# Two chained cross-attentions: layer-0 queries in blocks of 4, 8, 8, 6 and 6 subtiles instead of four blocks of 8

## The chip, the core and the metric

The kernel runs on one core of a Trainium2 chip. The metric is the device time of one execution in microseconds (us). A core has a matrix engine (PE in the profile, with its weight loads as PEld), a vector engine (DVE), an activation engine (ACT), GpSimd (POOL) and SyncE (SP), which here issues nearly all transfers. Each engine executes its own list of instructions in order and waits on semaphores; 16 DMA engines move data between DRAM and on-chip memory.

## The reference, cut to what matters

```python
# x: (4, 1024, 1024), context: (4, 64, 1024), all float32
# layer 0: 32 query heads of 32, 8 key/value heads
q = x @ Wq + bq; k = ctx @ Wk + bk; v = ctx @ Wv + bv
scores = einsum(q, k) / sqrt(32) + mask
out = softmax(scores) @ v
x1 = layernorm(out @ Wo + bo + x) * gamma + beta
# layer 1: 16 heads of 64, keys and values from layernorm(ctx)
Q = x1 @ Wq1.T; K = a @ Wk1.T; V = a @ Wv1.T
out = softmax(where(mask, Q K^T / 8, -inf)) @ V
y = x1 + tanh(gate) * (out @ Wo1.T)
```

There are 4096 query rows. The context is so short (256 rows in all) that layer 1 never forms Q: the keys are multiplied into Wq1 (the "folding of queries": matrices `ad`, one per batch) and the values into Wo1 (matrices `bd`), and layer 1 is then two 1024-by-1024 products per row.

## The kernel before, in words

**Units.** A subtile is 128 query rows; there are 32 (`NSUB`). A block is 8 subtiles (`SUB`), so 1024 rows, and there are 4 blocks (`NBLK`). Every large product is done by a Strassen-like scheme with 7 half-size products in place of 8: the left matrix is held as A11, A12, A22 and sums S1 to S4, the right as B11, B21, B22 and T1, T2, T3, N4.

**Layer-0 queries of one block.** `rows0(blk)` turns the rows of x into the 7 right-hand pieces of a block, each 512 columns wide: 8 DVE transposes (`turn_quarters`, L376) from the row buffers `xq`, then 4 DVE sums (L170 to L173). It returns three steps that are hung behind steps 22, 25 and 26 of the block before ("fills"). `query_steps(blk, rows)` gives 28 steps, 4 output slices times 7 products; a product is 4 matmuls at L536 (each shown by the profile as 2 rows). `keep` copies a PSUM bank to SBUF with the bias on ACT (L544), `add` adds a second bank on DVE (L550), and `put` sends the slice to DRAM (`qTd`, L547, on the SP queue). The SBUF tiles that `keep` writes (`e`, `z`, `u`, `f`) have two buffers each.

**Layer-0 attention of one subtile.** `attend0(t)` loads the queries of the subtile back from `qTd` (L593) and does, in two halves, scores (PE, L604), scaling and mask (DVE, L609), row maxima, subtraction, exponent (DVE L453 and L461, ACT L462), sums and division (DVE L471, L472, L476). `outputs0(t)` transposes the probabilities (PE L633, ACT L634), multiplies by the values (PE L639, ACT L643) and writes the result to `oTd` in DRAM (L645). A subtile can start only when the whole of its block's queries is in `qTd`.

**Mixing.** `mix(t, others)` writes the attention of subtile t, the outputs of subtile t-1 and a few other steps among each other. Block 0's queries are computed alone. After that the attention of block b is mixed with the 28 query steps of block b+1, 3 or 4 steps to a subtile: one step at each of four places, the rest behind the values.

```python
    for blk in range(NBLK - 1):
        steps = query_steps(blk + 1, rows)
        ...
        for i in range(SUB):
            lo, hi = i * 7 // 2, (i + 1) * 7 // 2
            mix(blk * SUB + i, steps[lo:hi] if i < SUB - 1 else steps[lo:])
```

The attention of the last block is mixed with the folding of layer-1 queries, one of 8 chunks to a subtile (`folded_queries`: a transposed weight chunk, PE L370 and ACT L371; 16 matmuls, L737; 8 evictions on ACT, L743; two writes of 1 MB to `ad`, L749). The chunk, its transpose and the two results take buffers from a ring of 7 (`wb`). The same stretch loads Wo of layer 0 and makes its sums (`w_o_sums`). This stage is called the fold stage below; the three before it are called mixed stages 0, 1 and 2.

**What follows.** 16 pairs of subtiles go through Wo and layer 1 (`project`, L400). For each pair `load_outputs` fetches the attention outputs from `oTd` (L782) and the residual rows, and `left_out` makes the sums S1 to S4 of them.

**Order.** The program gives each step in the order of the text; a scheduler then orders every engine's instructions by its own estimate of when their inputs are ready, and the order is fixed from there. So an engine can stand at an instruction whose input is late while a later one would be ready. Rows of x are loaded through `more_rows`: four row buffers for the first two blocks, two for the later ones, refilled as they come free, on the same SP queue as `put`.

Of the kernel before, what the change touches and what calls it, by code (L numbers as in the profile page):

```python
# [8 lines left out]
F32 = mybir.dt.float32  # L9
U8 = mybir.dt.uint8  # L10
AF = mybir.ActivationFunctionType
# [9 lines left out]
L = 1024  # L21
S = 64
NTOK = B * L
SUB = 8
TB = SUB * P
HT = TB // 2
NSUB = NTOK // P
NBLK = NTOK // TB
NPAIR = NSUB // 2
Q = 32  # L30
NQ = P // Q
# [35 lines left out]
def tile_two_cross_attentions(  # L67
# [47 lines left out]

    x1 = [dram.tile([2 * P, H], F32, tag=f"x1_{t}", name=f"x1_{t}") for t in range(NPAIR)]
    p1 = [dram.tile([2 * P, H], F32, tag=f"p1_{t}", name=f"p1_{t}") for t in range(NPAIR)]
    oTd = [dram.tile([P, KC, 2 * P], F32, tag=f"oT_{t}", name=f"oTd_{t}") for t in range(NPAIR)]
    qTd = [dram.tile([P, KC, TB], F32, tag=f"qT_{t}", name=f"qTd_{t}") for t in range(NBLK)]
    v0d = dram.tile([B * S, 256], F32, tag="v0d", name="v0d")  # L120
    kTd = dram.tile([P, KC, B * S], F32, tag="kTd", name="kTd")
    vTd = dram.tile([P, KC, B * S], F32, tag="vTd", name="vTd")
# [108 lines left out]
        for a in range(NQ):  # L231
            queue.dma_start(out=t[a * Q : (a + 1) * Q], in_=v[a])

    order = [(blk, i) for blk in range(NBLK) for i in range(4)]
    ahead = []
    free = [4, 2]

    def more_rows():

        while order and free[order[0][0] > 1]:  # L240
            blk, i = order.pop(0)
            free[blk > 1] -= 1
            xq = xpools[blk > 1].tile([P, 2 * NQ, QW], F32, tag="x", name=f"xq{blk}_{i}")
            at = blk * TB + i * 2 * P
            load_quarters(xq, x[at : at + 2 * P, :])
            ahead.append(xq)

# [132 lines left out]

    def left_out(o, pool, name):

        a11, a21 = o[:, 0:HK, 0:P], o[:, 0:HK, P : 2 * P]
        a12, a22 = o[:, HK:KC, 0:P], o[:, HK:KC, P : 2 * P]
# [5 lines left out]
        return {"A11": a11, "A12": a12, "A22": a22, "S3": a21, **s}  # L390

    def project(a, w, r, fill, bias=None, tail=None):

# [102 lines left out]
    def rows0(blk):  # L496

        r = {
            n: new_block("wb", f"x{n}_{blk}") for n in ("B11", "B21", "T1", "B22", "T3", "T2", "N4")
        }  # L500

        sums = right_sums(r)
        taken = []

        def turn_into(name, xq, i, h):
            at = slice(i % 2 * 2 * P, (i % 2 + 1) * 2 * P)
            turn_quarters(xq, r[name][:, :, at], (h * HK, (h + 1) * HK))

        def first_half():
            for i in range(2):  # L510
                xq = ahead.pop(0)
                turn_into("B11", xq, i, 0)
                turn_into("B21", xq, i, 1)
                done_with_rows(blk)

        def b12():
            for i in range(2, 4):
                taken.append(ahead.pop(0))
                turn_into("T1", taken[-1], i, 0)
            sums[0]()  # L520

        def b22():
            for i in range(2, 4):
                turn_into("B22", taken.pop(0), i, 1)
                done_with_rows(blk)
            run(sums[1:])

        return r, {22: first_half, 25: b12, 26: b22}

    def query_steps(blk, rows):  # L530

        tmp = {}

        def product(bank, a, b, i, first, last):
            for k in range(HK):
                nc.tensor.matmul(  # L536
                    bank, w_q[a][:, k, sub_ap(i)], rows[b][:, k, :],
                    start=first and k == 0, stop=last and k == HK - 1, skip_group_check=True,
                )

        def keep(name, bank, i, h):
            t = tmp[name] = etmp.tile([P, HT], F32, tag=name, name=f"{name}_{blk}_{i}")
            m = h * HK + i
            nc.scalar.activation(t, bank, AF.Identity, bias=bq_sb[:, m : m + 1])  # L544

        def put(name, i, h, u):
            nc.sync.dma_start(out=qTd[blk][:, h * HK + i, u * HT : (u + 1) * HT], in_=tmp[name])  # L547

        def add(name, bank, i, h, u):
            nc.vector.tensor_tensor(tmp[name], bank, tmp[name], ALU.add)  # L550
# [38 lines left out]
    def attend0(t):  # L589

        b = t * P // L
        q = qpool.tile([P, KC, P], F32, tag="q", name=f"q0_{t}")
        nc.sync.dma_start(out=q, in_=qTd[t // SUB][:, :, sub_ap(t % SUB)])  # L593
# [26 lines left out]
    def outputs0(t):  # L620
# [15 lines left out]
        def values(c):  # L636
            ps = one()
            for i in range(2):
                nc.tensor.matmul(  # L639
                    ps[i * 64 : (i + 1) * 64, :], v0bd[:, b, c, i, :], pTs[c][:, i, :],  # L640
                    start=True, stop=True,
                )
            nc.scalar.copy(oT[:, c * 4 : (c + 1) * 4, :].rearrange("p g l -> p (g l)"), ps)  # L643
            if c == 1:
                nc.sync.dma_start(out=oTd[t // 2][:, :, sub_ap(t % 2)], in_=oT)  # L645

        return flip, values

    def mix(t, others):

        front, back = attend0(t)
        o = iter(others)

        def other():
            step = next(o, None)
            if step:
                step()

        front(0)
        other()  # L660
# [11 lines left out]
        if t:  # L672
            values(0)
            values(1)
        for step in o:
            step()

    rows, fills = rows0(0)
    run(fills.values())
# [15 lines left out]
    for blk in range(NBLK - 1):  # L695
        steps = query_steps(blk + 1, rows)
        if blk + 2 < NBLK:
            rows, fills = rows0(blk + 2)

            def both(n, fills=fills, steps=steps):  # L700
                steps[n]()
                if n in fills:
                    fills[n]()

            steps = [lambda n=n: both(n) for n in range(28)]
        for i in range(SUB):
            lo, hi = i * 7 // 2, (i + 1) * 7 // 2
            mix(blk * SUB + i, steps[lo:hi] if i < SUB - 1 else steps[lo:])
    queries_cm.close()


# [66 lines left out]
        return [lambda bp=bp: keys(bp) for bp in range(2)]  # L778

    def load_outputs(pair):  # L780
        o = (o2pool if pair else early).tile([P, KC, 2 * P], F32, tag="o2", name=f"o2_{pair}")
        nc.sync.dma_start(out=o, in_=oTd[pair])  # L782
        r = []
        for u in range(2):
            t = pair * 2 + u
            ru = (rpool.tile([P, H], F32, tag="r", name=f"r_{t}") if pair
                  else early.tile([P, H], F32, tag="r", name=f"r_{t}", bufs=2))
            nc.sync.dma_start(out=ru, in_=x[sub_ap(t), :])
# [3 lines left out]

    kT = fold.tile([P, KC, B * S], F32, tag="kvT", name="kT")
    nc.sync.dma_start(out=kT, in_=kTd)
    wch = chunk(wq1, 0, "wq1")
    w_o, w_o_sums = right_weight(wo0, "wa", "wo0")
    bo_sb = constant(bo0.partition_broadcast(P), [P, H], "bo", F32, fold)
    for i in range(SUB):
        ahead = chunk(wq1, i + 1, "wq1") if i + 1 < KC else None
        mix((NBLK - 1) * SUB + i, folded_queries(kT, wch, i))  # L800
        wch = ahead
        if i == 3:
            run(w_o_sums)
        if i == 5:
            first_outputs = load_outputs(0)
    flip, values = outputs0(NSUB - 1)
    for part in (flip, values):
# [38 lines left out]
    def turn_x1(pair, xq, pool=None, tag="xT"):  # L846
# [4 lines left out]
            turn_quarters(xq, xT[:, h * HK : (h + 1) * HK, :], (h * HK, (h + 1) * HK))  # L851

        def blocks():
            lefts[pair] = left_out(xT, lpool if pool else lxpool, f"x_{pair}")

        return [lambda: half(0), lambda: half(1), blocks]

# [49 lines left out]
    def score(pair, fill):  # L907
        if pair:
            s = [spool.tile([P, H], F32, tag="s", name=f"s1_{pair}_{u}") for u in range(2)]
        else:  # L910
            both = o2pool.tile([P, 2, H], F32, tag="o2", name="s1_0")
            s = [both[:, u] for u in range(2)]
# [30 lines left out]
    def turn_at_once(pair):  # L943
        pT = new_pT(pair)
        del scores[pair]
        for u in range(2):
# [4 lines left out]
        return left_out(pT, lppool, f"p_{pair}")  # L951

    probs1 = {}
    at_once = {}
# [1 line left out]
    def turn_p(pair):  # L956
# [7 lines left out]
            turn_quarters(pq, pT[:, h * HK : (h + 1) * HK, :], (h * HK, (h + 1) * HK))  # L964

        def blocks():
            probs1[pair] = left_out(pT, lppool, f"p_{pair}")

        return [lambda: half(0), lambda: half(1), blocks]

# [93 lines left out]
```

## Time and profile before

| | us |
|---|---|
| median of 3 runs | 1969.04 (1968.19 to 1970.54) |
| the profiled execution, its own time | 1970.75 |
| its span in the trace | 1969.0 |
| start: context, keys and values | 0 to 83.1 |
| block 0's queries alone, up to block 1's first product | 83.1 to 178.0 |
| mixed stage 0 (8 subtiles, 28 steps of block 1) | 178.0 to 330.2 |
| mixed stage 1 | 330.2 to 482.1 |
| mixed stage 2 | 482.1 to 629.5 |
| fold stage (8 subtiles, 8 chunks) | 629.5 to 749.4 |
| Wo of layer 0 and layer 1 | 749.4 to 1969.0 |

The stage bounds are the starts of the first product of the next block, and in the last two rows the end of the last query product and the first product at L400. The profiled execution took 1.7 us more than the median run and its span is 1.75 us under its own time; a change of the span can be carried to the median as it is. Matrix products dominate, PE is busy in 98% of the span; but an engine can be busy and yet wait in small pieces, so the stages have to be read one by one.

### The profile page before, as it was taken

To read this page: it belongs to the slowest core of one execution; us is meant where nothing else is said; L and a number is where in the kernel's file an instruction comes from. 1 tells how busy PE (TensorE), PEld (TensorE's weight loads), DVE (VectorE), ACT (ScalarE), POOL (GpSimd) and SP (SyncE) were. 2 spreads that over 40 slices of the span, in tenths; PEclk is the share of its full clock that TensorE was granted. 3 is DMA by queue.
4 is the path that set the end of the run, shared out by engine and by line. 5 is a ranking of instruction groups with operands and counts; after the bars stand their busy time and mean duration, and the time that the engine had idled before them with its cause. 6 is when DMAs were issued, how large, how long until landed. Compare 5 with 4: busy or idle time off the path is not lost.

```text
span 1969.0 us, 16487 instructions
## 1 busy us (share of the span) xinstructions
PE 1929.0 (98%) x6208; PEld 922.9 (47%) x6208; DVE 1273.0 (65%) x1540; ACT 348.6 (18%) x564; POOL 237.6 (12%) x103
## 2 busy tenths in 40 slices
PE   8999999999999999999999999999999999999999
PEld 7744554444454664444443444444444444444443
DVE  3504968598877993455467667657675766576653
ACT  1011333243333672212200000000000000000000
POOL 0000000000000102445455643000000000000000
PEclk9999999999999899999999999999999999999999
DMA  8972226234425888376483335455746574747421
GB/s 276 181 178 71 90 82 161 72 110 120 128 89 192 278 268 288 136 238 226 157 247 119 118 109 126 139 145 154 181 118 161 138 181 118 179 120 181 118 86 43
DMA packets 204559, 301.17 MB, mean 153 GB/s; under 512 B 19136, under 2 KB 134208, under 8 KB 201920
## 3 DMA queue, kind: packets, MB, share of 16 engines
q1 hardware_dynamic: 185216, 270.75, 48.1%
q10 hardware_dynamic: 19264, 29.37, 5.4%
q8 instruction: 49, 0.80, 0.2%
q14 instruction: 30, 0.25, 0.0%
HBM read 182.37 MB, written 117.70 MB: 152 GB/s over the span
## 4 chain that ended last, share of the span: by engine, by line
PE 89%; DVE 8%; DMA 1%; issue 1%; ACT 1%; SPq 0%; DVEq 0%; ACTq 0%
PE wx L400 58%; PE wx L536 17%; PE big L604 2%; PE one L639 2%; PE one L633 2%; DVE s L609 1%; PE wx L350 1%; PE one L350 1%; DVE mx L453 1%; DVE s L461 1%; PE one L764 1%; DVE sm L471 1%; DVE s L476 1%; PE wx L737 1%; PE big L764 1%
## 5 line engine op out<-in xcount | busy, mean ns | idle before, releaser
L408 DVE TENSOR_TENSOR r<-wx,r 128x512 f32<-128x512 f32 x224 | 153.9, 687 | 269.3 <-PE wx L400 262.7
L462 ACT ACTIVATE s<-s 128x1024 f32<-128x1024 f32 x96 | 101.7, 1060 | 748.0 <-DVE s L461 739.3
L789 POOL TENSOR_TENSOR r<-r,bo 128x1024 f32<-128x1024 f32 x32 | 79.1, 2476 | 820.6 <-DMA r<-in_x_dram 819.5
L412 DVE TENSOR_TENSOR s<-wx,key_bias 128x512 f32<-128x512 f32 x64 | 44.2, 690 | 136.9 <-PE wx L400 136.9
L471 DVE TENSOR_REDUCE sm<-s 128x16 f32<-128x1024 f32 x96 | 115.2, 1211 | 22.0 <-ACT s L462 21.5
L536 PE MATMUL wx<-xT,wq_S 128*128 128x512 f32 x256 | 118.9, 605 | 3.1 <-DVE xT L171 3.1
L400 PE MATMUL wx<-wo_B,S 128*128 128x512 f32 x256 | 117.0, 599 | 0.7 <-DVE r L408 0.7
L536 PE MATMUL wx<-xB,wq_A 128*128 128x512 f32 x256 | 117.4, 599 | 0.0
L461 DVE TENSOR_TENSOR s<-s,mx 128x1024 f32<-128x1024 f32 x96 | 116.4, 1213 | 1.1
L453 DVE TENSOR_REDUCE mx<-s 128x16 f32<-128x1024 f32 x96 | 115.5, 1204 | 1.0
L400 PE MATMUL wx<-b_B,pT 128*128 128x512 f32 x256 | 116.1, 593 | 0.0
L400 PE MATMUL wx<-b_B,S_p 128*128 128x512 f32 x256 | 116.0, 596 | 0.0
L400 PE MATMUL wx<-a_B,xT 128*128 128x512 f32 x256 | 115.4, 592 | 0.0
L400 PE MATMUL wx<-a_B,S_x 128*128 128x512 f32 x256 | 115.3, 593 | 0.0
L476 DVE TENSOR_TENSOR s<-s,sm 128x1024 f32<-128x1024 f32 x92 | 113.3, 1240 | 0.9
L400 PE MATMUL wx<-wo_B,o 128*128 128x512 f32 x256 | 113.8, 595 | 0.0
L609 DVE SCALAR_TENSOR_TENSOR s<-big,m 128x1024 f32<-128x1024 f32 x64 | 77.9, 1217 | 31.6 <-PE big L604 31.5
L830 POOL TENSOR_TENSOR r<-r,gamma 128x1024 f32<-128x1024 f32 x32 | 76.1, 2377 | 140.9 <-DVE r L280 140.9
L604 PEld LDWEIGHTS big<-kv,q 64*128 64x128 f32 x1024 | 67.0, 191 | 45.2 <-issue 23.0
L604 PE MATMUL big<-kv,q 64*128 64x128 f32 x1024 | 80.3, 290 | 5.7 <-DMA q<-qTd 2.9
L831 POOL TENSOR_TENSOR r<-r,beta 128x1024 f32<-128x1024 f32 x32 | 80.9, 2528 | 2.4
L634 ACT COPY pT<-one 128x512 f32<-128x512 f32 x128 | 69.3, 595 | 55.9 <-PE one L633 55.7
(152 smaller groups left out, 2689.3 us busy)
## 6 DMA issues: line engine op xcount, KB each, us to landing
xq<-in_x_dram SPq DMA_DIRECT2D x64, 256.0 KB, 9.1
q<-qTd SPq DMA_DIRECT2D x32, 512.0 KB, 4.2
oTd<-oT SPq DMA_DIRECT2D x32, 512.0 KB, 3.6
o<-oTd SPq DMA_DIRECT2D x16, 1024.0 KB, 8.6
ad<-a SPq DMA_DIRECT2D x16, 1024.0 KB, 6.4
r<-in_x_dram SPq DMA_DIRECT2D x32, 512.0 KB, 4.3
bd<-b SPq DMA_DIRECT2D x32, 512.0 KB, 6.6
x<-r SPq DMA_DIRECT2D x32, 512.0 KB, 2.9
```

What stands on the lines that cost most here:

```text
L400: nc.tensor.matmul(bank, a[s][:, k, :], w[m][:, k, :], start=first and k == 0, stop=last and k == HK - 1, skip_group_check=True,)
L408: nc.vector.tensor_tensor(at, bank, at, ALU.add)
L453: r = nc.vector.tensor_reduce(mx, s, AX.X, ALU.max)
L461: nc.vector.tensor_tensor(s, s, mx.unsqueeze(2).to_broadcast([P, 16, S]), ALU.subtract)
L462: nc.scalar.activation(s, s, AF.Exp)
L471: nc.vector.tensor_reduce(sm, s, AX.X, ALU.add)
L476: nc.vector.tensor_tensor(s, s, sm.unsqueeze(2).to_broadcast([P, 16, S]), ALU.mult)
L536: nc.tensor.matmul(bank, w_q[a][:, k, sub_ap(i)], rows[b][:, k, :], start=first and k == 0, stop=last and k == HK - 1, skip_group_check=True,)
L604: nc.tensor.matmul(ps[:, at : at + P], q[on, c * 4 + g, :], k0bd[on, b, c, :], start=True, stop=True,)
L609: nc.vector.scalar_tensor_tensor(s, ps.rearrange("p (h s) -> p h s", h=16), SCALE0, m.unsqueeze(1).to_broadcast([P, 16, S]), ALU.mult, ALU ...
L789: nc.gpsimd.tensor_tensor(ru, ru, bo_sb, ALU.add)
L831: nc.gpsimd.tensor_tensor(r[u], r[u], beta0_sb, ALU.add)
```

## The change

Blocks get sizes of their own, `SUBS = (4, 8, 8, 6, 6)`, so there are five, and every place that took 8 subtiles to a block takes its size from there. A block of 4 has pieces 256 columns wide and one of 6 has 384; the products, evictions, adds and writes of `qTd` are that narrow, and their number per block stays. Where a half of a block is not a whole number of row buffers (6 subtiles: 3 and 3), a buffer is turned in two parts.

`mix` has five places for other steps and deals the steps out evenly over what places are left. The attention over the 28 query steps is thus 4 subtiles (7 steps each) over block 1, 8 over block 2, 8 over block 3 and 6 over block 4. The fold stage is the last 6 subtiles: the 8 chunks are cut into 6 steps each (a load of the chunk after it, then five), and the 48 steps are dealt out 8 to a subtile. The sums of Wo come behind the third subtile of the six, the first outputs are loaded behind the fourth.

`oTd` is one DRAM tile per subtile instead of per pair, so the write of a subtile's outputs is 4 KB in a run per partition instead of 512 bytes; a pair is read by two loads of 512 KB instead of one of 1 MB, and `left_out` takes a list of two views.

```diff
-SUB = 8
-TB = SUB * P
-HT = TB // 2
+SUBS = (4, 8, 8, 6, 6)
+NBLK = len(SUBS)
+FIRST = [sum(SUBS[:n]) for n in range(NBLK)]
...
-    oTd = [dram.tile([P, KC, 2 * P], F32, ...) for t in range(NPAIR)]
+    oTd = [dram.tile([P, KC, P], F32, ...) for t in range(NSUB)]
...
-    order = [(blk, i) for blk in range(NBLK) for i in range(4)]
+    order = [(blk, i) for blk in range(NBLK) for i in range(SUBS[blk] // 2)]
...
     def rows0(blk):
         r = {
-            n: new_block("wb", f"x{n}_{blk}") for n in (...)
+            n: new_block("wb", f"x{n}_{blk}")[:, :, 0 : SUBS[blk] * P // 2]
+            for n in (...)
         }
+        half = SUBS[blk] // 2
+        taken = {}
+        def turn_into(n, u, h):
+            for i in range(u * half // 2, -(-(u + 1) * half // 2)):
+                if i not in taken:
+                    taken[i] = ahead.pop(0)
+                lo, hi = max(2 * i, u * half), min(2 * i + 2, (u + 1) * half)
+                turn_quarters(...)
+                if h and hi == 2 * i + 2:
+                    del taken[i]
+                    done_with_rows(blk)
...
     def query_steps(blk, rows):
+        width = SUBS[blk] * P // 2
...
-            t = tmp[name] = etmp.tile([P, HT], F32, tag=name, ...)
+            t = tmp[name] = etmp.tile([P, 512], F32, tag=name, ...)[:, 0:width]
...
             if c == 1:
-                nc.sync.dma_start(out=oTd[t // 2][:, :, sub_ap(t % 2)], in_=oT)
+                nc.sync.dma_start(out=oTd[t], in_=oT)
...
     def mix(t, others):
-        o = iter(others)
+        others = list(others)
+        places = 5
         def other():
-            step = next(o, None)
-            if step:
-                step()
+            nonlocal places
+            for _ in range(-(-len(others) // places)):
+                others.pop(0)()
+            places -= 1
...
-        for i in range(SUB):
-            lo, hi = i * 7 // 2, (i + 1) * 7 // 2
-            mix(blk * SUB + i, steps[lo:hi] if i < SUB - 1 else steps[lo:])
+        n = SUBS[blk]
+        for i in range(n):
+            mix(FIRST[blk] + i, steps[i * 28 // n : (i + 1) * 28 // n])
...
+    def fold_chunk(k):
+        steps = []
+        def load():
+            if k + 1 < KC:
+                ahead.append(chunk(wq1, k + 1, "wq1"))
+            steps.extend(folded_queries(kT, ahead.pop(0), k))
+        return [load] + [lambda n=n: steps[n]() for n in range(5)]
+
+    folds = [f for k in range(KC) for f in fold_chunk(k)]
+    n = SUBS[-1]
+    for i in range(n):
+        mix(FIRST[-1] + i, folds[i * len(folds) // n : (i + 1) * len(folds) // n])
-        if i == 3:
+        if i == n // 2 - 1:
             run(w_o_sums)
-        if i == 5:
+        if i == n - 3:
             first_outputs = load_outputs(0)
```

More of the change, by code (lines that the diff above doesn't have):

```diff
@@ L23 @@
 NTOK = B * L
-SUB = 8
-TB = SUB * P
-HT = TB // 2
 NSUB = NTOK // P
-NBLK = NTOK // TB
+SUBS = (4, 8, 8, 6, 6)
+NBLK = len(SUBS)
+FIRST = [sum(SUBS[:n]) for n in range(NBLK)]
 NPAIR = NSUB // 2
@@ L117, in tile_two_cross_attentions @@
     p1 = [dram.tile([2 * P, H], F32, tag=f"p1_{t}", name=f"p1_{t}") for t in range(NPAIR)]
-    oTd = [dram.tile([P, KC, 2 * P], F32, tag=f"oT_{t}", name=f"oTd_{t}") for t in range(NPAIR)]
-    qTd = [dram.tile([P, KC, TB], F32, tag=f"qT_{t}", name=f"qTd_{t}") for t in range(NBLK)]
+    oTd = [dram.tile([P, KC, P], F32, tag=f"oT_{t}", name=f"oTd_{t}") for t in range(NSUB)]
+    qTd = [
+        dram.tile([P, KC, SUBS[t] * P], F32, tag=f"qT_{t}", name=f"qTd_{t}") for t in range(NBLK)
+    ]
     v0d = dram.tile([B * S, 256], F32, tag="v0d", name="v0d")
@@ L243, in more_rows @@
             xq = xpools[blk > 1].tile([P, 2 * NQ, QW], F32, tag="x", name=f"xq{blk}_{i}")
-            at = blk * TB + i * 2 * P
+            at = (FIRST[blk] + i * 2) * P
             load_quarters(xq, x[at : at + 2 * P, :])
@@ L381, in left_out @@
     def left_out(o, pool, name):
-        a11, a21 = o[:, 0:HK, 0:P], o[:, 0:HK, P : 2 * P]
-        a12, a22 = o[:, HK:KC, 0:P], o[:, HK:KC, P : 2 * P]
+        a11, a21 = o[0][:, 0:HK], o[1][:, 0:HK]
+        a12, a22 = o[0][:, HK:KC], o[1][:, HK:KC]
         s = {n: pool.tile([P, HK, P], F32, tag=n, name=f"{n}_{name}") for n in ("S1", "S2", "S4")}
@@ L390, in left_out, with both @@
         return {"A11": a11, "A12": a12, "A22": a22, "S3": a21, **s}
+    def both(o):
+        return [o[:, :, 0:P], o[:, :, P : 2 * P]]
     def project(a, w, r, fill, bias=None, tail=None):
@@ L498, in rows0 @@
         r = {
-            n: new_block("wb", f"x{n}_{blk}") for n in ("B11", "B21", "T1", "B22", "T3", "T2", "N4")
+            n: new_block("wb", f"x{n}_{blk}")[:, :, 0 : SUBS[blk] * P // 2]
+            for n in ("B11", "B21", "T1", "B22", "T3", "T2", "N4")
         }
         sums = right_sums(r)
[L503 to L507, printed above, removed]
-        def first_half():
[L510 to L514, printed above, removed]
+        half = SUBS[blk] // 2
[5 more added lines that the diff above has]
+                lo, hi = max(2 * i, u * half), min(2 * i + 2, (u + 1) * half)
+                turn_quarters(
+                    taken[i][:, (lo - 2 * i) * NQ : (hi - 2 * i) * NQ, :],
+                    r[n][:, :, (lo - u * half) * P : (hi - u * half) * P], (h * HK, (h + 1) * HK),
+                )
+                if h and hi == 2 * i + 2:
+                    del taken[i]
+                    done_with_rows(blk)
+        def first_half():
+            turn_into("B11", 0, 0)
+            turn_into("B21", 0, 1)
         def b12():
-            for i in range(2, 4):
-                taken.append(ahead.pop(0))
-                turn_into("T1", taken[-1], i, 0)
+            turn_into("T1", 1, 0)
             sums[0]()
         def b22():
-            for i in range(2, 4):
-                turn_into("B22", taken.pop(0), i, 1)
-                done_with_rows(blk)
+            turn_into("B22", 1, 1)
             run(sums[1:])
@@ L536, in product @@
                 nc.tensor.matmul(
-                    bank, w_q[a][:, k, sub_ap(i)], rows[b][:, k, :],
+                    bank[:, 0:width], w_q[a][:, k, sub_ap(i)], rows[b][:, k, :],
                     start=first and k == 0, stop=last and k == HK - 1, skip_group_check=True,
@@ L541, in keep @@
         def keep(name, bank, i, h):
-            t = tmp[name] = etmp.tile([P, HT], F32, tag=name, name=f"{name}_{blk}_{i}")
+            t = tmp[name] = etmp.tile([P, 512], F32, tag=name, name=f"{name}_{blk}_{i}")[:, 0:width]
             m = h * HK + i
-            nc.scalar.activation(t, bank, AF.Identity, bias=bq_sb[:, m : m + 1])
+            nc.scalar.activation(t, bank[:, 0:width], AF.Identity, bias=bq_sb[:, m : m + 1])
         def put(name, i, h, u):
-            nc.sync.dma_start(out=qTd[blk][:, h * HK + i, u * HT : (u + 1) * HT], in_=tmp[name])
+            nc.sync.dma_start(out=qTd[blk][:, h * HK + i, u * width : (u + 1) * width], in_=tmp[name])
         def add(name, bank, i, h, u):
-            nc.vector.tensor_tensor(tmp[name], bank, tmp[name], ALU.add)
+            nc.vector.tensor_tensor(tmp[name], bank[:, 0:width], tmp[name], ALU.add)
             put(name, i, h, u)
@@ L591, in attend0 @@
         b = t * P // L
+        blk = max(n for n in range(NBLK) if FIRST[n] <= t)
         q = qpool.tile([P, KC, P], F32, tag="q", name=f"q0_{t}")
-        nc.sync.dma_start(out=q, in_=qTd[t // SUB][:, :, sub_ap(t % SUB)])
+        nc.sync.dma_start(out=q, in_=qTd[blk][:, :, sub_ap(t - FIRST[blk])])
         m = small.tile([P, S], F32, tag="m0", name=f"m0_{t}")
@@ L674, in mix @@
             values(1)
-        for step in o:
-            step()
+        other()
     rows, fills = rows0(0)
@@ L698, in tile_two_cross_attentions, with step_and_fill @@
             rows, fills = rows0(blk + 2)
-            def both(n, fills=fills, steps=steps):
+            def step_and_fill(n, fills=fills, steps=steps):
                 steps[n]()
@@ L703, in both @@
                     fills[n]()
-            steps = [lambda n=n: both(n) for n in range(28)]
-        for i in range(SUB):
-            lo, hi = i * 7 // 2, (i + 1) * 7 // 2
-            mix(blk * SUB + i, steps[lo:hi] if i < SUB - 1 else steps[lo:])
+            steps = [lambda n=n: step_and_fill(n) for n in range(28)]
+        n = SUBS[blk]
+        for i in range(n):
+            mix(FIRST[blk] + i, steps[i * 28 // n : (i + 1) * 28 // n])
     queries_cm.close()
@@ L780, in load_outputs @@
     def load_outputs(pair):
-        o = (o2pool if pair else early).tile([P, KC, 2 * P], F32, tag="o2", name=f"o2_{pair}")
-        nc.sync.dma_start(out=o, in_=oTd[pair])
-        r = []
+        o, r = [], []
+        pool = o2pool if pair else early
+        o2 = pool.tile([P, 2, KC, P], F32, tag="o2", name=f"o2_{pair}")
         for u in range(2):
             t = pair * 2 + u
+            o.append(o2[:, u])
+            nc.sync.dma_start(out=o[u], in_=oTd[t])
             ru = (rpool.tile([P, H], F32, tag="r", name=f"r_{t}") if pair
@@ L794, in tile_two_cross_attentions @@
     nc.sync.dma_start(out=kT, in_=kTd)
-    wch = chunk(wq1, 0, "wq1")
+    ahead = [chunk(wq1, 0, "wq1")]
     w_o, w_o_sums = right_weight(wo0, "wa", "wo0")
     bo_sb = constant(bo0.partition_broadcast(P), [P, H], "bo", F32, fold)
[L798 to L801, printed above, removed]
-        if i == 3:
+    def fold_chunk(k):
[10 more added lines that the diff above has]
+        if i == n // 2 - 1:
             run(w_o_sums)
-        if i == 5:
+        if i == n - 3:
             first_outputs = load_outputs(0)
@@ L853, in blocks @@
         def blocks():
-            lefts[pair] = left_out(xT, lpool if pool else lxpool, f"x_{pair}")
+            lefts[pair] = left_out(both(xT), lpool if pool else lxpool, f"x_{pair}")
         return [lambda: half(0), lambda: half(1), blocks]
@@ L910, in score @@
         else:
-            both = o2pool.tile([P, 2, H], F32, tag="o2", name="s1_0")
-            s = [both[:, u] for u in range(2)]
+            s0 = o2pool.tile([P, 2, H], F32, tag="o2", name="s1_0")
+            s = [s0[:, u] for u in range(2)]
         project(lefts.pop(pair), w_a, s, fill, key_bias[:, pair // PPB, :])
@@ L950, in turn_at_once @@
             )
-        return left_out(pT, lppool, f"p_{pair}")
+        return left_out(both(pT), lppool, f"p_{pair}")
     probs1 = {}
@@ L966, in blocks @@
         def blocks():
-            probs1[pair] = left_out(pT, lppool, f"p_{pair}")
+            probs1[pair] = left_out(both(pT), lppool, f"p_{pair}")
         return [lambda: half(0), lambda: half(1), blocks]
```

## The prediction

> **What bounds the kernel now.** I read the page first (shares, chain), then the engines' busy time by stage, then the timelines where stages meet, then the DMA rows.
>
> ```profile
> PE 1929.0 (98%) x6208; PEld 922.9 (47%) x6208; DVE 1273.0 (65%) x1540; ACT 348.6 (18%) x564; POOL 237.6 (12%) x103
> ...
> PE 89%; DVE 8%; DMA 1%; issue 1%; ACT 1%; SPq 0%; DVEq 0%; ACTq 0%
> ```
>
> PE carries the chain, but DVE takes 8% of it, and in the table by stage one sees where. Columns: length, then busy time of PE, PEld, DVE, ACT, POOL, then the granted clock, DMA share and GB/s.
>
> ```profile
> 83.10:178.00 94.90, 91.76 (x209) 39.75 (x208) 29.29 (x25) 9.99 (x15) 0.00 (x0) 0.98 0.53 127
> ...
> 330.20:482.10 151.90, 149.01 (x675) 74.32 (x673) 119.89 (x122) 53.56 (x80) 0.00 (x0) 1.00 0.41 110
> ...
> 629.50:749.40 119.90, 108.27 (x810) 72.63 (x809) 105.93 (x105) 84.93 (x152) 5.64 (x2) 0.94 0.84 269
> ...
> 690.00:740.00 50.00, 46.27 (x388) 32.24 (x386) 48.95 (x50) 39.99 (x74) 0.00 (x0) 1.00 0.82 266
> ```
>
> Block 0 alone leaves DVE idle for 65 us; the fold stage has DVE busy in 48.95 of 50 us. The softmax of a subtile recurs there every 12.41 us:
>
> ```profile
> 692.98 1.23 DVE L609 SCALAR_TENSOR_TENSOR s<-big,m 128x1024 f32<-128x1024 f32 x1
> ...
> 705.40 1.22 DVE L609 SCALAR_TENSOR_TENSOR s<-big,m 128x1024 f32<-128x1024 f32 x1
> ```
>
> Moving two subtiles from the fold to stages where PE is the limit is what the change can win.
>
> **Unit prices.** From the chain:
>
> ```profile
> 45.28 3.45 PE one L350 x16
> ...
> 266.95 3.44 PE wx L536 x8
> ...
> 341.83 26.14 PE wx L536 x60
> ```
>
> A product 512 wide (8 rows) is 3.44 us. L350 is 256 wide: 16 rows in 3.45, so half of it per row. Hence 28 products cost 96.3 us for a block of 8, 72.2 for 6, 48.2 for 4. Between the T2 products at 266.78 and 303.60 in PE's timeline lie two subtiles and 7 products: 36.82 - 24.1 = 12.7, or 6.4 us of PE per subtile where PE is the limit. [...] The L350 row says +0 (3.45 against 2 x 3.44 / 2), in this very kernel and type, so I take 0.
>
> **The change part by part** (profiled 1970.75, span 1969.0; the difference goes to the median unchanged).
>
> *Block 0, 4 subtiles.* Before: from 83.1 to the end of its last product at 185.95, less 0.86 for two rows of block 1: 102.0 us for 96.3 of products. Most of the rest is here, where the row buffers came late and the clock was low behind the gap (5.20 us for 8 rows):
>
> ```profile
> 93.28 5.20 PE L536 MATMUL wx<-xT,wq_S 128*128 128x512 f32 x8 [3.14 <-DVE xT L171]
> ...
> 90.01 22.44 SPq L232 DMA_DIRECT2D xq<-in_x_dram  x23
> ...
> 116.15 0.32 SPq L547 DMA_DIRECT2D qTd<-e  x1
> ```
>
> And in the DMA rows of that stretch (KB, median us to landing):
>
> ```profile
> qTd<-e SPq DMA_DIRECT2D x2, 256.0 KB, 10.3
> ```
>
> After: two row buffers are enough, both turned by 77; four half-size sums (2.25 to 1.15 each) end at 82, so that 4.6 us wait goes. But a new one comes. The first `put` stood on SP behind the row loads and landed at 126.5; nobody waited, since its tile was wanted again at 140 (third slice). Now 15 loads of 256 KB follow 90.0 instead of 23: at the 200 GB/s of that stretch they end near 112, then kTd and vTd (2 MB at some 410 GB/s) near 117, and the put behind them. The third slice's `keep` wants the tile at 83.1 + 15 x 1.72 + 1 = 110; PE has three more products, to 115; ACT frees the bank at 117.5. So 2.5 us of idle, with the low clock after it 3.5 (bounds 0 and 9: landing early or after all 6 MB). After: 48.2 + 1 + 3.5 = 52.7. Change -49.3.
>
> *Mixed stage 0, 4 subtiles over block 1.* The same 28 products, four subtiles fewer: -25.6. Queries of subtile 0 are asked for 8 matmuls (6.9 us) after the last product, instead of 11 (9.5, which held); last product to scores needs add, put and load, 7.4 us: 0.5 lost. Block 1's fills (18.4 us of DVE) stand in front of that add in DVE's order, 13 us in all, which fits into the 13.8 us that PE takes over the same steps. Change -25.
>
> *Mixed stage 1, 8 over 8.* PE's order is the old one: 30 matmuls (26.14 above) in which DVE waits for new queries, then attention at DVE's rate. Fills are a quarter smaller, but its late part is PE's. Change 0.
>
> *Mixed stage 2, 8 over 6.* Here PE has only 72.2 + 51.2 = 123.4 us of work and DVE 8 x 11.6 to 12.4 (the rate in the catch-up after 372 and in the fold) + adds 6 + fills 14 = 113 to 119, and in the new order 31 matmuls of 0.645 and two transposes and the values come before the first scores: 23.6 us without softmax work. Walking both orders with the durations above, the stage takes 23.6 + 105 = 128.7, and DVE is 12 us behind at its end. Before 147.4: change -18.7.
>
> *New mixed stage 3, 6 over 6.* 72.2 + 6 x 6.4 = 110.6, +3.3 since the T2 product and the next queries (z add, put, load) wait for the backlog of DVE, +1.1 at the first transposes: 115.
>
> *Fold stage, 6 subtiles, 8 chunks.* Before: 11.4 us to the first softmax (last product, add, put 2.1, load 4.6, scores), 89.3 for seven intervals, 19.2 of tail: 119.9. If DVE's 12.41 stayed the limit: 11.4 + 5 x 12.41 + 19.2 = 92.7. But a subtile now carries 1.33 chunks. PE: scores 2.2, transposes 1.7, values 1.9, folding 5.1 x 1.33: 12.6 plus its small waits (0.9 now). ACT: 7.9 of 10 us now, so 9.8 per subtile; +1.6 is 11.4. DMA: 0.82 x 12.41 = 10.2 us per subtile, `ad` and the weight chunk a third more: 12.5. Four engines within 1 us of each other, chained through one score bank and a ring of 7 buffers. In the new DVE order subtiles 28, 30 and 31 sum (L471) directly after the subtraction, so DVE stands for the exponent on ACT, twice each, 1.2 us: where the old order had an independent step in that place (the L471 at 702.69 in the timeline waited 0.1). 5.0 in the intervals, 2.5 in the tail. I take 13.6 per interval from PE's and DVE's walk, tail 22, +3 for DMA landing later: 104.5 (bounds 92.7 and 118). Change -15.4.
>
> *The rest.* 12 more adds and 16 more `keep`s, narrower: DVE +1.7, in stages counted above. 16 more puts at 0.32 on SP, beside PE. `oTd` in 4 KB runs: a write lands in 3.6 us and nobody waits for it but loads much later: 0. 16 more loads of outputs on SP (0.5 each) in a stage of 1219.6 us at DMA share 0.53: 0; PE's order from L400 on is the old one. Wo's sums still run before the last add (L173 ended at 634.3): 0. If that cover goes, 2.3 a sum.
>
> Sum: -49.3 - 25 + 0 - 18.7 + 115 - 15.4 = +6.6; the single roundings run against me, so +6: 1969.04 + 6 = 1975.
>
> **The rivals.**
> *The fold stays with DVE (faster).* One mechanism: PE, ACT and DMA keep their chunk work in the shade of the softmax, at under 12.4 us per subtile, and the exponent is hidden. For it: PE was idle 3.7 of 50 us, ACT 10. Against: the sums 12.6 and 12.5 above. The fold is then 93 to 95, 10.5 less: 1964.5. It decides from 12.7 per interval and tail 20 on, where the whole is level with before.
> *DMA is the fold's limit (much slower).* The buffers of a chunk are wanted again two chunks later; chunks now follow in under 10 us, and `ad` writes landed in 4.4 to 11.5. ACT standing at a transposed chunk holds up the exponents. Share 0.82 speaks for it, the shorter runs gone from `oTd` against. Per interval 15 to 16: 1987.
> [...]
>
> **How the numbers follow.** Forecast 0.47 (1970 to 1981), fold with DVE 0.25, DMA limit 0.25, narrow 0.03. About 0.2%, 3.9 us, is what a measurement of this kernel can tell from no change: 1965.1 to 1972.9. Faster by more: half of the DVE case and a little, for missed gains in the stages before, 0.21. Within: the rest of that case and the low end of the forecast, 0.18. Slower: 0.61. The range 1962 to 1990 takes in the DVE case but its lower end and the DMA case but its upper end; the forecast's own is 1970 to 1981.
>
> **What would show it.** In the profile after: block 0 without the 3.14 us wait for L171 but with ACT's third `e` near 117; first scores near 145; the third mixed stage near 129 with DVE over 9 tenths; five L609 intervals of the fold at 13 to 14 us with PE's idle small and DVE's waits ended by ACT's exponent; the layer-1 stage at 1219.6 as before. Wrong if the fold's intervals are 12.4 or above 15, if products of 256 or 384 columns take more than 1.72 or 2.58 us, or if the stage from the first L400 product moves by over 3 us.

## The result, and the profile after

The changed kernel takes 1987.06 us (median of 4 runs, 1984.41 to 1990.42) against 1969.79 for the kernel before in the same series: ratio 1.0089, interval 1.0071 to 1.0108. So it is slower by 17 us. The forecast was +6, 1975, with 1970 to 1981 as its own range; the whole range, which took in the rivals, went from 1962 to 1990. The sign held, and so did the whole range, but not the forecast's own. The size was 11 us short, which is the miss in one stage; the misses elsewhere cancel.

The page of the profile after: span, busy time, and the chain by engine.

```profile
span 1985.8 us, 17065 instructions
...
PE 1937.2 (98%) x6432; PEld 966.9 (49%) x6432; DVE 1270.4 (64%) x1560; ACT 355.4 (18%) x580; POOL 237.1 (12%) x103
...
PE 62%; DVE 3%; issue 0%; ACT 0%; ACTq 0%; DVEq 0%
```

The page alone hides the matter: PE is at 98% as before, and this chain could be followed through only 65% of the span. The busy times by stage show it (columns as in the table before: length, PE, PEld, DVE, ACT, POOL, granted clock, DMA share, GB/s). The stages are: block 0's queries with mixed stage 0, mixed stages 1, 2 and 3, fold, Wo and layer 1.

```profile
82.43:260.16 177.73, 170.90 (x650) 99.74 (x648) 87.77 (x90) 37.72 (x60) 0.00 (x0) 0.98 0.40 105
260.16:411.90 151.74, 148.85 (x673) 74.17 (x671) 122.77 (x124) 52.97 (x79) 0.00 (x0) 1.00 0.38 111
411.90:541.72 129.82, 126.47 (x675) 74.92 (x673) 109.14 (x118) 51.23 (x80) 0.00 (x0) 1.00 0.35 106
541.72:653.73 112.01, 111.75 (x564) 66.15 (x563) 91.17 (x93) 41.42 (x65) 0.00 (x0) 1.00 0.45 152
653.73:769.17 115.44, 97.91 (x688) 66.40 (x686) 79.09 (x79) 75.96 (x134) 5.65 (x2) 0.91 0.77 259
769.17:1985.80 1216.63, 1205.64 (x2840) 519.59 (x2840) 747.68 (x1013) 85.83 (x138) 228.95 (x94) 1.00 0.53 152
```

The fold ends at the first product of Wo that stands behind the last attention, at 769.17; its counterpart before is the mark at 749.4 (a few products of L400 are interleaved ahead of it in both kernels, from 742.6 before and 762.4 after). Against the forecast:

| stretch | before | after | forecast change | measured change |
|---|---|---|---|---|
| start | 83.1 | 82.4 | 0 | -0.7 |
| block 0 and mixed stage 0 | 247.1 | 177.7 | -74.3 | -69.4 |
| mixed stage 1 | 151.9 | 151.7 | 0 | -0.1 |
| mixed stage 2 | 147.5 | 129.8 | -18.7 | -17.6 |
| mixed stage 3 (new) | | 112.0 | +115 | +112.0 |
| fold | 119.9 | 115.4 | -15.4 | -4.5 |
| Wo and layer 1 | 1219.6 | 1216.6 | 0 | -3.0 |

Two terms are off by more than 3 us: the fold by 11, block 0 with its mixed stage by 5. In the fold the granted clock is 0.91 (0.94 before) and DVE, busy for 105.93 of 119.90 us before, is busy for only 79.09 of 115.44: the softmax no longer sets the pace, and PE's 97.91 leave 17.5 us of stops. The softmax of a subtile starts here (first half of each of the six subtiles, DVE's timeline; in brackets the wait before and what ended it):

```profile
663.78 1.23 DVE L620 SCALAR_TENSOR_TENSOR s<-big,m 128x1024 f32<-128x1024 f32 x1 [6.43 <-PE big L615]
...
674.93 1.21 DVE L620 SCALAR_TENSOR_TENSOR s<-big,m 128x1024 f32<-128x1024 f32 x1
...
690.03 1.23 DVE L620 SCALAR_TENSOR_TENSOR s<-big,m 128x1024 f32<-128x1024 f32 x1 [1.61 <-PE big L615]
...
708.76 1.23 DVE L620 SCALAR_TENSOR_TENSOR s<-big,m 128x1024 f32<-128x1024 f32 x1 [1.67 <-PE big L615]
...
728.91 1.22 DVE L620 SCALAR_TENSOR_TENSOR s<-big,m 128x1024 f32<-128x1024 f32 x1 [7.79 <-PE big L615]
...
746.18 1.23 DVE L620 SCALAR_TENSOR_TENSOR s<-big,m 128x1024 f32<-128x1024 f32 x1 [2.65 <-PE big L615]
```

Intervals of 11.2, 15.1, 18.7, 20.2 and 17.3: 82.4 us for five, where the forecast had 68 and the kernel before would have taken 62. The last four starts each wait for PE's scores. PE in turn stands 17.5 us in this stage, and the list of its waits says for whom (650 to 762 us; in total, times, longest):

```profile
PE one L644 <- ACT wq1T L372: 5.3, 3, 2.1
PE one L650 <- ACT pT L645: 4.0, 3, 2.6
PE big L615 <- DVE s L620: 3.7, 3, 1.6
PE big L615 <- DMA q<-qTd: 2.3, 1, 2.3
PE one L371 <- ACT pT L645: 1.4, 1, 1.4
```

Most of it is for ACT's copies; one stop of 2.3 us, ahead of the first scores, is for a DMA. One case lies between 716 and 729. PE's timeline:

```profile
716.65 1.09 PE L644 MATMUL one<-ident,s 128*128 128x128 f32 x8
717.67 0.49 PE L615 MATMUL big<-kv,q 64*128 64x128 f32 x4
720.80 3.68 PE L650 MATMUL one<-pT,kv 128*64 128x512 f32 x8 [2.63 <-ACT pT L645]
```

and ACT's:

```profile
717.27 1.06 ACT L466 ACTIVATE s<-s 128x1024 f32<-128x1024 f32 x1 [0.76 <-DVE s L465]
718.23 2.04 ACT L755 ACTIVATE a<-wx 128x512 f32<-128x512 f32 x4
720.14 1.10 ACT L645 COPY pT<-one 128x512 f32<-128x512 f32 x2
```

The transposed probabilities are in their bank at 717.7, but ACT first does an exponent that had waited for DVE, then four copies of folded results, and only then the copy that the values need. PE stands for 2.63 us. The 3.68 us of the next row, 1.94 elsewhere, is the second half of the price: the clock, which the trace shows at 0.50 from 695.77 to 702.60 and from 719.66 to 729.90. Cut into pieces of 3.41 us (columns: length, PE busy, granted clock, DMA share, GB/s):

```profile
678.70:682.12 3.42, 1.91 (x16) 1.00 1.02 274
682.12:685.53 3.41, 2.78 (x20) 1.00 1.11 349
...
688.95:692.36 3.41, 3.41 (x46) 1.00 0.74 282
692.36:695.77 3.41, 1.33 (x13) 1.00 0.99 288
695.77:699.18 3.41, 3.41 (x12) 0.50 1.03 391
699.18:702.60 3.42, 3.42 (x14) 0.50 0.49 137
702.60:706.01 3.41, 3.39 (x23) 1.00 0.51 193
...
712.84:716.25 3.41, 3.41 (x26) 1.00 0.60 179
716.25:719.66 3.41, 1.92 (x16) 1.00 0.94 291
719.66:723.08 3.42, 2.28 (x6) 0.50 0.99 372
723.08:726.49 3.41, 3.41 (x12) 0.50 0.45 171
726.49:729.90 3.41, 3.41 (x21) 0.50 0.22 88
729.90:733.32 3.42, 3.42 (x42) 1.00 0.06 20
```

The piece in which PE was busy for 1.33 of 3.41 us is followed by two pieces at half clock, and one with 1.92 by three. But another with 1.91 (at 678.70) is followed by full clock, so the busy time of one piece doesn't decide alone. The 8 rows of L650 took 3.68 us at a granted 0.50 (720.80) against 1.94 at 1.00 (704.82), and PE counts as busy through both, so "busy 98%" says little here.

### The profile page after: what moved, and what is told of

Its sections match the earlier page's. It is cut to its first block, busy times and chain, and to the rows that moved or that the text cites. A ratio compares the mean times of both kernels' runs of the same rounds, so it can differ in the third digit from the quotient of the medians.

```text
span 1985.8 us, 17065 instructions
## 1 busy us (share of the span) xinstructions
PE 1937.2 (98%) x6432; PEld 966.9 (49%) x6432; DVE 1270.4 (64%) x1560; ACT 355.4 (18%) x580; POOL 237.1 (12%) x103
## 4 chain that ended last, share of the span: by engine, by line
PE 62%; DVE 3%; issue 0%; ACT 0%; ACTq 0%; DVEq 0%
PE wx L404 58%; PE one L776 1%; PE big L776 1%; PE one L650 1%; PE wx L749 1%; DVE s L465 0%; DVE mx L457 0%; DVE s L620 0%; PE one L644 0%; PE big L615 0%; PE one L371 0%; DVE sm L475 0%; DVE S L388 0%; ACT a L755 0%; DVE S L387 0%
## 5 line engine op out<-in xcount | busy, mean ns | idle before, releaser
L546 PE MATMUL wx<-xT,wq_S 128*128 128x384 f32 (+2 forms) x320 | 123.1, 524 | 4.9 <-ACT e L554 4.9
L546 PE MATMUL wx<-xB,wq_A 128*128 128x384 f32 (+2 forms) x320 | 120.0, 514 | 0.0
L404 PE MATMUL wx<-a_B,xT 128*128 128x512 f32 x256 | 115.4, 592 | 0.0
L546 PEld LDWEIGHTS wx<-xT,wq_S 128*128 128x128 f32 x320 | 59.2, 193 | 47.3 <-issue 25.5
```

The costliest lines, as they stand in the source:

```text
L404: nc.tensor.matmul(bank, a[s][:, k, :], w[m][:, k, :], start=first and k == 0, stop=last and k == HK - 1, skip_group_check=True,)
L546: nc.tensor.matmul(bank[:, 0:width], w_q[a][:, k, sub_ap(i)], rows[b][:, k, :], start=first and k == 0, stop=last and k == HK - 1, skip_gr ...
```

## The experiments

For the fold of each kernel the length is split into three terms: PE's stops (length less PE's busy time), the loss by half clock (half of the time granted at 0.5, an estimate from the 3.68 us for 1.94 above), and the rest, PE's work at full clock. (A stop inside a half-clock piece counts in both, which makes the work up to 1.1 us too small; kernels with the same products differ by up to 3.5 us in this column, so read no more than that from it.) The whole times are medians, each beside the kernel before in the same series (1968.6 to 1970.3).

| kernel | whole | ratio, interval | fold | work | half-clock loss | stops |
|---|---|---|---|---|---|---|
| before | 1969.79 | | 119.7 | 101.2 | 6.8 | 11.6 |
| changed | 1987.06 | 1.0089 (1.0071 to 1.0108) | 115.4 | 87.7 | 10.2 | 17.5 |
| no_split | 1971.69 | 1.0006 (0.9998 to 1.0014) | 121.3 | 101.2 | 5.1 | 15.0 |
| fold8 | 1986.79 | 1.0087 (1.0074 to 1.0100) | 115.9 | 100.5 | 3.4 | 12.0 |
| e4 | 1987.74 | 1.0089 (1.0074 to 1.0103) | 119.3 | 86.6 | 13.6 | 19.1 |
| pair_out | 1992.84 | 1.0116 (1.0101 to 1.0131) | 120.9 | 87.6 | 15.4 | 17.9 |
| ad_more | 1995.20 | 1.0128 (1.0113 to 1.0143) | 119.4 | 87.5 | 12.0 | 20.0 |
| turn_wx | 1984.05 | 1.0073 (1.0057 to 1.0088) | 113.9 | 84.4 | 6.8 | 22.6 |
| half_fold | 1974.21 | 1.0020 (1.0012 to 1.0027) | 101.1 | 72.6 | 8.5 | 20.0 |
| deal_late | 1981.78 | 1.0063 (1.0049 to 1.0076) | 110.3 | 87.9 | 6.8 | 15.5 |
| filler | 2000.76 | 1.0163 (1.0149 to 1.0177) | 131.1 | 102.4 | 12.0 | 16.8 |
| both | 1976.37 | 1.0036 (1.0023 to 1.0048) | 104.6 | 86.1 | 5.1 | 13.4 |
| all_three | 1974.12 | 1.0024 (1.0014 to 1.0034) | 104.0 | 86.6 | 3.4 | 13.9 |
| no_split_wx | 1969.96 | 1.0005 (0.9997 to 1.0014) | 118.8 | 100.0 | 5.1 | 13.7 |

In the fold the change took 13.5 us of work from PE, and stops (+5.9) and clock (+3.4) gave 9.3 of it back.

**no_split: the parts other than the block sizes.**

```diff
-SUBS = (4, 8, 8, 6, 6)
+SUBS = (8, 8, 8, 8)
```

> SUBS = (8, 8, 8, 8), all else as changed (steps of the folding dealt out one by one, outputs by whole subtile). Theory A, the 11 us over the forecast come from carrying 8 chunks on only 6 subtiles: with one chunk to a subtile the fold goes back to about 12.4 us per subtile and the whole to 1969, between 1965 and 1973. Rival B, the new dealing costs whatever the number of subtiles (exponents and transposed chunks in a worse order on ACT): fold intervals of 14 us and more, whole 1980 or above.

Level with before; the last five intervals of its fold are 12.4 us each. The new dealing and the whole-subtile outputs cost nothing measurable with one chunk to a subtile. Rival B falls; the loss comes with the block sizes.

**fold8: five blocks, but 8 subtiles in the fold.**

```diff
-SUBS = (4, 8, 8, 6, 6)
+SUBS = (4, 8, 6, 6, 8)
```

> SUBS = (4, 8, 6, 6, 8): five blocks and a first one of 4 as changed, but 8 subtiles for the 8 chunks. Theory A: the fold takes about 120 us at 12.4 per subtile, with granted clock near full; the stages of queries sum from the changed kernel's own to 121.7 (4 over 8), 129.8 (8 over 6), 112 (6 over 6) and about 140 (6 over 8), so some 8 us under the changed kernel: 1979 (1975 to 1983). Rival C, five blocks cost of themselves, one more change of stage: the query stages are longer by what the fold gains, 1987 or more.

The fold behaves (its last four intervals are 12.4 us, 3.4 us are lost to the clock) but the whole is where the changed kernel is, so theory A in this form falls. The stage of 6 subtiles over a block of 6 took 118.1 us, not 112, and that of 6 over 8 took 145.3, not 140: in the latter PE stood 3.1 us for a sum of rows (L172) and 2.3 for a `keep`, with 6.8 us at half clock. So with these sizes the stages of queries lost what the fold gained, as rival C has it; that five blocks cost by themselves is not shown, since the order of the sizes changed too.

**e4: block 0 without its wait for a write.**

```diff
-            t = tmp[name] = etmp.tile([P, 512], F32, tag=name, ...)[:, 0:width]
+            if name == "e" and blk == 0 and i > 1:
+                t = etmp.tile([P, 256], F32, tag="e0", ...)
+            else:
+                t = etmp.tile([P, 512], F32, tag=name, ...)[:, 0:width]
+            tmp[name] = t
```

> As changed, but slices 2 and 3 of block 0 keep their first bank in two tiles of their own, so they need not wait for the first writes of queries to land. Theory: the wait of 4.9 us of PE in block 0 and the half clock behind it (1.7 us) go, and the end of block 0 and all after it come 6 us earlier: 1981 (1979 to 1983). Rival: the next tile (z or u of slice 2) takes its place with a wait of about the same end, 1986 to 1988.

In the changed kernel ACT's third `e` waits for the first write of queries, and PE for it (ACT's and PE's timelines):

```profile
118.03 0.47 ACT L554 ACTIVATE e<-wx,bq 128x256 f32<-128x256 f32 x1 [11.62 <-DMA qTd<-e]
```

```profile
118.56 3.47 PE L546 MATMUL wx<-xT,wq_S 128*128 128x256 f32 x8 [4.88 <-ACT e L554]
```

With the tiles of their own that wait is gone, and both pieces of half clock before block 2 with it; a shorter one of 2.56 us takes its place, for DVE's sum into `u` at 127.6, as the rival had it in part. From block 0's first product to block 2's first is 173.2 us, not 177.7, so 4.5 of the 6 us. The whole did not move, 1987.74 with runs from 1982.57 to 1992.06: this profile's fold is 3.9 us longer, 3.4 of it half clock. Taken alone, a gain of 4.5 us can't be told from the fold's spread.

**pair_out: outputs to DRAM by pair, as before.**

```diff
...
-                nc.sync.dma_start(out=oTd[t], in_=oT)
+                nc.sync.dma_start(out=oTd[t // 2][:, :, sub_ap(t % 2)], in_=oT)
...
```

> As changed, but the attention outputs go to DRAM by pair with 512 byte runs, as before. Theory: nobody waits for these writes, within 2 us of the changed kernel (1985 to 1989), stages equal within 1 us but for the fold, which moves by its half clock windows. Rival, the shorter runs crowd the queues in the fold: 1992 or more and landings of the outputs above 4 us.

1992.84, the rival's number, 6 us over the changed kernel, though the intervals of the two ratios overlap a little. The writes of the fold land in 3.9 us (3.5 with whole subtiles), not above 4, and the fold's work is the same; 5.1 of its 5.5 us are half clock. Since e4, which writes whole subtiles, has 3.4 us more of half clock than the changed kernel too, these profiles don't show that the short runs are the cause.

**ad_more: 4 MB more to DRAM in the fold.**

```diff
...
+                nc.gpsimd.dma_start(
+                    out=ad_again[:, sub_ap(k), n * 512 : n * 512 + 128].rearrange("b p o -> p b o"),
+                    in_=st[n][:, :, 0:128],
+                )
```

> As changed, with 4 MB of extra writes in the fold: a quarter of every folded result goes a second time to DRAM, to a place nobody reads, from GpSimd's queue, so that the other queues and PE, DVE and ACT keep their order. At the changed kernel's 0.78 share over 107 us that is some 10 us more of DMA time. Theory, the fold is held up by engines that wait for each other in order and not by DMA: fold stage (last query product to first product of Wo) within 3 us of the changed kernel's 108.7 and the whole 1985 to 1991. Rival, DMA sets the pace: fold +8 to +10, whole 1995 or more.

The whole (+8.1) is the rival's, the fold lies between: +4.0, where the extra queue took 10.4% of 119.4 us on the 16 DMA engines, 12.4 us. The softmax intervals are 12.8, 19.9, 16.9, 19.1 and 17.3 us: the first two grew by 1.6 and 4.8, the next two shrank by 1.8 and 1.1, and the last is the same. In the changed kernel the first two have a DMA share of 1.04 and 0.99, but their growth doesn't show that transfers hold them: e4, without any transfer added, has 13.2 and 19.0 there. So extra transfers do cost in this kernel; that they set the pace of the fold does not follow, and the waits speak against it: in the changed kernel's fold one stop of PE, 2.3 us, ended with a DMA, in ad_more two, 3.9 us. (One wait of ACT, 2.5 us at 678.31, has no ender in the profile.) The other 4 us of the whole fall in small pieces outside the fold, 2.6 of them in layer 1.

**half_fold and filler: less and more work for PE.**

```diff
-        st = [wpool.tile([P, B, 512], F32, tag="wb", ...) for n in range(2)]
+        st = [wpool.tile([P, B, 512], F32, tag="wb", ...) for n in range(1)]
...
         def heads(cc):
+            if cc > 1:
+                if cc == 3:
+                    write(1, 0)
+                return
...
```

> Half of the folding is left out: of each chunk only the first 512 columns are multiplied and copied out, and are written to both halves, so DRAM traffic stays and PE loses 1.9 us and ACT 2 us per chunk. Theory: with PE and ACT work per subtile back under that of the kernel before, the softmax interval returns to 12.4 to 13 us, half clock windows to 3 or fewer, the fold to 92 to 96 and the whole to about 1972. Rival, DMA sets the pace: interval stays at 16, whole 1985 or more.

```diff
         def values(c):
             ps = one()
+            if t >= FIRST[-1] - 1:
+                nc.tensor.matmul(
+                    ps, ident, kT[:, 0:2, :].rearrange("p k s -> p (k s)"), start=True, stop=True
+                )
```

> As changed, with more PE work: in the last seven subtiles a matmul of 128 x 512 that depends on nothing late (identity times keys, overwritten at once) goes into the bank ahead of each product with the values, 14 in all, 12 us of PE at full clock; the order of the engines is else all but the same. [...] Rival, PE's work per subtile sets the pace: fold +9 to +12, whole 1996 or more.

With the same traffic to DRAM and half of the folding, the whole falls to 1974.21 and three of the five intervals are 11.6 to 11.9 us. With DMA as the limit throughout, all would have stayed at 16. One is 23.1, though, in which PE stood 2.58 us for ACT's copy of probabilities and 2.33 for a load of queries, and in it the DMA share is 1.00:

```profile
700.63:723.69 23.06, 16.28 (x112) 11.25 (x110) 13.30 (x15) 13.00 (x23) 3.52 (x2) 0.88 1.00 345
```

So transfers are not out as the limit of a single interval. half_fold also takes copies from ACT and one of the two result buffers from the ring, so it can't tell PE's work from these; filler adds to PE alone. It answers the other way than I had expected, which was a fold moved by -3 to +4 us with most of the filler inside the stops: 28 rows of 0.43 us, 12 us of extra PE work, did not disappear in the stops but lengthened the fold by 15.7 us (work +14.7, stops -0.7, clock +1.8), and half_fold took 15.1 us of work out and got 14.3 shorter. So PE's work counts at least one for one in this stage, though PE stands for 17 us of it: I read the stops as latencies of PE, ACT and DVE waiting for each other in turn, which come on top of the work and do not overlap it.

**turn_wx, deal_late and both: fewer stops for ACT.** The first takes the transposed chunks through the large PSUM banks, the second deals the 8 steps 2, 1, 1, 1, 3, the third does both.

```diff
-            turn(wch, lambda h: wT[:, h * HK : (h + 1) * HK, :])
+            turn(wch, lambda h: wT[:, h * HK : (h + 1) * HK, :], [wx(), wx()])
```

> As changed, but the transposed weight chunks of the folding go through two of the four large PSUM banks instead of the two small banks which the transposed probabilities and the values also use. Theory: PE's stops for ACT's copies (L372 and L645 ended 11 us of PE's idle time in the fold) fall by half, with fewer windows of half clock: fold 102 to 105, whole 1980 to 1984. Rival, DMA or DVE's own chain holds the fold: 1985 to 1989, or slower if the folding products now wait for their banks.

```diff
-            for _ in range(-(-len(others) // places)):
+            few = 2 if places == 5 else 1
+            for _ in range((few if places > 1 else len(others)) if late else -(-len(others) // places)):
                 others.pop(0)()
...
```

> As changed, but the 8 folding steps of a subtile are dealt 2, 1, 1, 1 and 3 over its five places instead of 2, 2, 2, 1, 1, so fewer copies of folded results stand on ACT ahead of the transposed probabilities. Theory, ACT's order makes PE stop: fold 3 to 6 us shorter, whole 1981 to 1984. Rival, the load per subtile alone counts: 1986 to 1989; the long run of folding at the end can also make the next scores late, 1990.

> The changed kernel with the late dealing (2, 1, 1, 1, 3) and the transposed chunks through the large banks together. If the two gains add (3.0 and 5.3 us of the whole): 1978 to 1980, fold near 101. If they cure the same stops: 1981 to 1983.

Alone they give 3.0 and 5.3 us (the interval of each overlaps that of the changed kernel, the second barely), together 10.7, which is clear of it. That this is more than the sum is within the noise. turn_wx moved the stops rather than removed them (22.6 us), but lost 3.4 us less to the clock. Together (the kernel both), the fold, cut half a us wider than in the table, and its five softmax intervals are

```profile
652.10:757.20 105.10, 91.70 (x690) 62.73 (x689) 78.90 (x79) 73.73 (x134) 5.72 (x2) 0.95 0.86 285
...
660.95:733.00 72.05, 62.13 (x501) 43.43 (x501) 60.51 (x61) 52.72 (x95) 5.72 (x2) 0.96 0.95 313
```

with PE's work at 86.1 us (87.7 in the changed kernel), DMA share up to 0.86, and clock up to 0.95. What differs from the changed kernel is the order of the steps and the banks of one kind of transpose: 10.8 us of the fold were a matter of these, with all transfers as they were. Over the five intervals the DMA share is now 0.95; whether transfers are the next limit was not tried.

**all_three and no_split_wx: is there a better kernel?** The first adds e4's tiles to the kernel above; the second is no_split with the banks of turn_wx and steps dealt 1, 1, 1, 1, 2.

> As the kernel with late dealing and large banks, plus the two extra tiles of block 0. Its block 0 is 4 us shorter by the trace seen before; theory, that is a real gain which was lost in the fold only by where its half clocks fell: 3 to 5 us under the kernel without it (1974 to 1977). Rival, the next stage gives it back always: equal to it within 1.5 us.

> SUBS = (8, 8, 8, 8), steps dealt 1, 1, 1, 1, 2, transposed chunks through the large banks: the kernel before with what helped in the fold. There DVE holds the fold at 12.4 us per subtile whatever PE and ACT do, so no more than 1 to 2 us from fewer half clocks: 1968 to 1971, level with before. If the banks' turnover counted there too: 1964 to 1967, under both kernels.

all_three is 2.3 us under the kernel without the tiles, less than expected and with overlapping intervals, and by its ratio 4.7 us over the kernel before. no_split_wx is level with before: the fold of 8 stays with DVE. None of the versions beats the kernel before.

## Why the prediction was right in sign and short in size

*Block sizes in the stages of queries.* Right in size: mixed stages 1, 2 and 3 within 3 us each. The steps are less so: DVE was busy for 0.84 of mixed stage 2 (109.14 of 129.82 us), not over 0.9, and the 4.4 us of waits in mixed stage 3 did not come (PE busy for 111.75 of 112.01 us). Narrow matmuls cost nothing extra here: in the stretch without waits the groups of eight 128x256 rows start at 97.97, 99.70 and 101.42, so 1.73 us each, half of the 3.44 of a full product; eight rows of 128x384 (426.15 to 428.73) take 2.58. That they cost more has 0.03 of the prediction's chances; no run shows such a cost. The 3.0 us of the last stretch are one piece of half clock less (3.4 us for 6.8, so 1.7) and a PE wait of 1.7 us at a product of L764 that the profile before has and the one after has not.

*Block 0.* The mechanism was right, the write that lands late, but its size was 2.5 us of wait and turned out at 4.88: the first write landed 12.2 us after its issue at 105.71. (Before, it had landed 11.6 us after its issue, at 127.7 and not 126.5: the 10.3 in the DMA row is the median of two writes. The argument does not hang on it.) Its half clock, put at 1 us, was 1.7; another half-clock piece at 149.6, behind 1.82 us of PE waiting for the first queries, cost as much again and was not in the sum: the first scores of a subtile came at 148.2, not near 145. With e4 this term is -73.9, against the -74.3 of the forecast.

*The fold: the step that failed.* "I take 13.6 per interval from PE's and DVE's walk" was 16.5, and by the prediction's own sign (above 15) the step is wrong. The five intervals came to 14.4 us over the forecast's 68; the first softmax was 1.4 us early, the tail 1.0 longer than its 22, and the 3 us set aside for late landings go against this: 11 in all. Over the five intervals (columns as above):

```profile
663.78:746.18 82.40, 70.48 (x505) 48.40 (x505) 61.19 (x61) 54.76 (x96) 5.65 (x2) 0.89 0.79 264
```

The loads "within 1 us of each other" were sized well: per interval PE has 12.3 us of work (70.48 less the 9.2 lost to half clock, by five), DVE 12.2, ACT 11.0 and DMA 13.0, where the prediction has 12.6, 12.4, 11.4 and 12.5. What failed is the sum over them: it allowed PE 0.9 us of small waits per subtile, as before, and gave the stops no price in clock. There were 2.4 us of stops and 1.8 of half clock per interval, 12.3 + 2.4 + 1.8 = 16.5. What the walk left out is how the engines of that order wait for each other: with another order and other banks (the kernel both) the fold is 104.6. That this meets the forecast's 104.5 is partly luck, since its intervals are 14.4 and not 13.6. The exposed exponents, to which the prediction gave 7.5 us, are there (9.0 us of DVE's waits, up to 3.23 a time), but the subtile with the longest interval, 20.2 us, is one whose DVE order had none.

*The rivals.* DMA as the fold's limit gave 1987 and 15 to 16 per interval, all but the measured numbers. Its mechanism shows in part only: PE did stand for ACT's transposed chunks (5.3 us), but no wait of ACT or DVE in the fold is put down to a DMA, and the kernel both gets 10.8 us back with all transfers in place. So it is luck that the whole range, which was drawn wide for this rival, took in the result. That the fold stays with DVE is out: DVE was busy for 79 of 115 us. That narrow matmuls cost more is out too.

*The clock.* In the fold no PE stop is longer than 2.63 us, and the granted clock shows 20.5 us at half. The half clock from 695.77 and that from 719.66 came behind pieces in which PE was busy for 1.33 and 1.92 of 3.41 us. That such stops cause it is my reading; no run held everything else fixed and moved PE's busy time alone, and turn_wx, with 22.6 us of stops, lost 6.8 us to the clock where the changed kernel, with 17.5, lost 10.2.

*Open:* whether the 512 byte runs cost the 5 us of clock in pair_out, by what way ad_more's transfers cost 8 us, and why fold8's stages of 6 over 6 and 6 over 8 lost 6 and 5 us.

## What to carry to other kernels

When a stage has four engines within a tenth of each other, don't price it by the busiest one: write down the order of the in-order engines through one period and add the latencies where one stands for another; here the order of steps and the choice of banks gave 10.8 us back. Price PE stops, as an estimate, at more than their length: in the folds of the 14 kernels the half-clock loss was 0.25 to 0.86 of the stops. A gain early in a kernel is seen in its stage, not in the whole, as long as a later stage spreads by several us from run to run.

## What the runs showed of the hardware

In the traces of the kernel before and of the changed one the granted clock is 1.00 or 0.50. In the fold before it is 0.50 for 13.7 us (3.4 from 639.08, 6.8 from 652.73, 3.4 from 669.80), in the changed kernel's for 20.5 us (3.4 from 661.64, 6.8 from 695.77, 10.2 from 719.66). In the 3.4 us ahead of each of the latter three PE was busy for 1.13, 1.33 and 1.92 us; the 1.91 us at 678.70, with full clock after it, stand against reading a limit from these. What sets the clock, and so what a single stop costs, was not shown. The changed kernel's runs have spans of 1982.0 to 1988.1 us at mean clocks of 0.993 to 0.990, and 0.003 of the span is 6 us: the clock's spread has the size of the spread in time.
